# Layer 0's keys, values and context moved into the checks, and layer 2's mixer bias folded into a row

## The chip, the cores and the metric

The kernel runs on one core of one Trainium2 chip. The metric is the device time of one execution in microseconds (us); lower is better. An execution is one launch that computes the whole four-layer network.

## The reference

A graph of 3125 nodes with 256 features each goes through four layers. A layer normalises x, adds a graph attention over some 100,000 edges and a linear "mixer" attention, and then adds a mixture-of-experts block. What matters here is layer 0's mixer and layer 2's sum:

```python
xn = _layernorm(x, axis=-1)
x = x + _L0_gnn_ref(xn, edge_index, ...) + _L0_mix_ref(xn[None], L0_mix_Wqkv, ...)[0]
...
xn = _layernorm(x, axis=-1)
x = x + _L2_gnn_ref(xn, edge_index, ...) + _L2_mix_ref(xn[None], L2_mix_Wq, L2_mix_Wkv, L2_mix_Wproj, L2_mix_bproj)[0]
```

`_L0_mix_ref` takes queries, keys and values from `xn @ Wqkv`, normalises the keys with a softmax over all nodes, forms one context matrix for each head from keys and values, applies it to the queries, multiplies by a gate (a small network on the layer-normalised xn) and projects. The softmax over nodes means that the context needs every node once before any output can be made. `_L2_mix_ref` ends in `einsum(out, Wproj) + bproj`, and `_L2_gnn_ref` ends in a LayerNorm, `... * gamma + beta`. Both are added to the same x.

## The kernel before

The nodes lie in 25 tiles of 125 on the partitions; `GROUPS` joins them to seven groups of four or three tiles. `xn` is the normalised x, `xT` its transpose (features on partitions).

The program has two versions of the network: a fast one (`layers`) and a general one (`general`). Which of the two runs is decided on the chip. `run` loads x, then `begin_layer` normalises all seven groups and transposes them, then `prepare` makes the checks: it counts, for each block of nodes, how many row heads lie before it (five compares over 3224 numbers, L1381), gathers the edge segments with five indirect DMAs on the POOL queue (L1387), builds low digits and keys, writes them to HBM (`seg_d`), tests the sorted edges, the size of the segments, the spread of the attention terms (the `p_e` matmuls over `xT` and the reductions at L1438 and L1439) and the size of Wk. The result is one number, `ok`. It is loaded into registers and a branch follows. What stands before the branch can't be mixed with what stands behind it.

Behind the branch, in `layers`, `counts` builds the matrix of edge counts in 63 steps. In each step DVE makes two one-hot tensors (`oh_lo` L1515, `oh_key` L1518), PE multiplies them (`p_cnt`, L1530, 20 matmuls), and ACT turns the result into bytes (`stage`, L1532), which every fifth step go to HBM (`count_d`, L1536). Beside these steps runs a generator, `mix0_pieces`, with the mixer of layer 0; at each `yield` it hands back. `counts` takes `PIECES0` pieces, spread evenly over the steps, and what is left after the last step follows at once:

```python
while done < (g0 // B + 1) * PIECES0 // steps:
    next(work, None)
    done += 1
```

The pieces before the change are: the weights with the bias add on POOL over the whole x (L1557), then one piece for each tile with its keys and values (`p_a` on PE, Exp and a copy on ACT, a memset of one column on POOL at L1567, and the context matmuls `p_ctx` at L1569), one piece that folds the context into the query weight (`fold`), six for each group (LayerNorm, transpose, gate, fold, projection), and then the node tables of the graph attention (`node_pieces`). That makes 107, which is also `PIECES0`. The dense attention (`dense_pairs`) follows; it reads `count_d` back.

The order on each engine is made by a scheduler at build time from the order in the text (earlier is more urgent) and from what is ready; on the chip each engine and each DMA queue then works in that fixed order. The PE order of the dense attention alone is written out by hand.

In layer 2, `mix2` runs beside the node tables: `keys_values` loops over the 25 tiles (`p_kvt`, `key`, `val`, `p_kv`), and behind it in the text stands the mixer's bias add over the whole x on POOL (L1138). Later `gnn2_out` adds the attention's part to x, with `beta` on POOL (L1120) from a row that `gnn2_weights` loads.

Of the kernel before, what the change touches and what calls it, by code (L numbers as in the profile page):

```python
# [41 lines left out]
KEYS = HI * GN  # L42
PIECES0 = 107
SC = 8
# [12 lines left out]
class Net:  # L57
# [1045 lines left out]
    def gnn2_weights(self, c):  # L1103
        return [self.row(c, "L2_gnn_" + n) for n in ("bias", "gamma", "beta")]

# [18 lines left out]
    def mix2(self, x, xn, xT, work=iter(())):  # L1124
        nc, tc = self.nc, self.tc
        with ExitStack() as s:
            c = s.enter_context(tc.tile_pool(name="m2", bufs=1))
            w = s.enter_context(tc.tile_pool(name="m2w", bufs=2))
            wq, wkv, wproj = (self.weight(c, "L2_mix_" + n) for n in ("Wq", "Wkv", "Wproj"))
            bproj = self.row(c, "L2_mix_bproj")  # L1130

            def finish(out, num, den, z):
                nc.vector.tensor_scalar(z, den, 1e-6, None, op0=OP.max)
                nc.vector.reciprocal(z, z)
                nc.vector.tensor_mul(out, num, z)

            kv, den = self.keys_values(c, w, x, xn, xT, wkv, work)
            nc.gpsimd.tensor_add(x, x, bproj[:, None, :].to_broadcast([TP, NT, C]))  # L1138
# [212 lines left out]
class Dense(Net):  # L1351
# [8 lines left out]
    def prepare(self, pool, xT):  # L1360
# [6 lines left out]
        with ExitStack() as s:  # L1367
# [60 lines left out]
            nc.vector.tensor_reduce(found[:, 1:2], above, AX.X, OP.add)  # L1428
            p_f = ps.tile([1, 2], F32, name="p_f")
            nc.tensor.matmul(p_f, self.ones[:, 0:1], found, start=True, stop=True)  # L1430


            gw = self.gnn_weight(w, ps, "g0", 8)
            ends = w.tile([16, 2, len(GROUPS)], F32, name="ends")
# [30 lines left out]
            nc.vector.tensor_mul(self.ok, ok[:, 0:1], ok[:, 2:3])  # L1465
        return self.ok

# [4 lines left out]
    def counts(self, pieces):  # L1472
# [5 lines left out]
        with ExitStack() as s:  # L1478
# [5 lines left out]
            with tc.tile_pool(name="cnti", bufs=1) as wi, tc.tile_pool(name="cntt", bufs=2, space=PSUM) as ps:  # L1484
                for i, name in enumerate(("lo_t", "key_t")):
# [57 lines left out]
    def mix0_pieces(self, x, xn, xT, nodes, c, w):  # L1543
# [3 lines left out]
        with ExitStack() as s:  # L1547
            ps = s.enter_context(tc.tile_pool(name="m0p", bufs=3, space=PSUM))
            ps1 = s.enter_context(tc.tile_pool(name="m0p1", bufs=1, space=PSUM))
            wqkv = self.weight(c, "L0_mix_Wqkv")  # L1550
            wproj = self.weight(c, "L0_mix_Wproj")
# [3 lines left out]
            bg1, bg2 = self.vec(c, "L0_mix_bg1", rows=64), self.vec(c, "L0_mix_bg2")  # L1555
            bproj = self.row(c, "L0_mix_bproj")
            nc.gpsimd.tensor_add(x, x, bproj[:, None, :].to_broadcast([TP, NT, C]))  # L1557
            p_ctx = [ps1.tile([P, P + 1], F32, name=f"p_ctx{m}") for m in range(KC)]
            yield
            for t in range(NT):  # L1560
                p = ps.tile([TP, 2 * C], F32, name="p_a")
                self.mm(p, [(xT[:, k, t * TP:(t + 1) * TP], wqkv[:, k, C:]) for k in range(KC)])
                ek = w.tile([TP, C], F32, name="ek", bufs=2)
                nc.scalar.activation(ek, p[:, :C], AF.Exp)
                v = w.tile([TP, KC, P + 1], F32, name="v", bufs=2)
                nc.scalar.activation(v[:, :, :P], p[:, C:].rearrange("p (m f) -> p m f", m=KC), AF.Copy)
                nc.gpsimd.memset(v[:, :, P], 1.0)  # L1567
                for m in range(KC):
                    nc.tensor.matmul(p_ctx[m], ek[:, m * P:(m + 1) * P], v[:, m, :], start=(t == 0), stop=(t == NT - 1))  # L1569
                yield  # L1570

            inv = w.tile([P, KC], F32, name="inv")
            ctxt = w.tile([P, KC, P], F32, name="ctxt")
            for m in range(KC):
                nc.vector.reciprocal(inv[:, m:m + 1], p_ctx[m][:, P:])
                nc.vector.scalar_tensor_tensor(ctxt[:, m, :], p_ctx[m][:, :P], inv[:, m:m + 1], self.heads, op0=OP.mult, op1=OP.mult)
            fold = c.tile([P, KC, C], F32, name="fold")
            for k in range(KC):
                p = ps.tile([P, 512], F32, name="p_a")
                for m in range(KC):  # L1580
                    nc.tensor.transpose(p[:, m * P:(m + 1) * P], wqkv[:, k, m * P:(m + 1) * P], self.ident)
                wt = w.tile([P, C], F32, name="wq_t")
                nc.vector.tensor_copy(wt, p[:, :C])
                p = ps.tile([P, 512], F32, name="p_a")
                for m in range(KC):
                    nc.tensor.matmul(p[:, m * P:(m + 1) * P], wt[:, m * P:(m + 1) * P], ctxt[:, m, :], start=True, stop=True)
                nc.vector.tensor_copy(fold[:, k, :], p[:, :C])
            yield
            for t0, nt in GROUPS:
# [876 lines left out]
    def run(self, x_in, out):  # L2466
# [195 lines left out]
```

## Time and profile before

| | us |
|---|---|
| median of 3 runs | 5535.72 (5531.63 to 5546.36) |
| the profiled execution | 5533.53 |
| its span in the trace | 5531.5 |

| stretch of the profiled execution, us | what runs |
|---|---|
| 0 to 32 | x arrives, LayerNorm and transposes |
| 32 to 93 | the checks, up to the branch |
| 93 to 385 | counts with the pieces; first count write issued at 143.4, last at 384.7 |
| 385 to 406 | the last write lands, the node tables are finished, the first loads of the dense attention land |
| 2929 to 3116 | layer 2's mixer beside its node tables |

"Busy" is the time in which an engine worked on an instruction. PE is TensorE, PEld its weight loads, DVE VectorE, ACT ScalarE, POOL GpSimd, SP the queue that issues most DMAs. Lines such as L1530 are lines of the kernel. A name before an arrow is what an instruction writes, the names behind it what it reads. "Granted clock" is the share of its full speed that TensorE was given. Times come from one profiled execution, and a matmul's own duration holds a fixed delay, so dense matmuls are counted by their spacing.

### The profile page before, as it was taken

The page shows a single profiled execution, that of the slowest core. Times are in us where ns is not written, and L with a number is a line of the kernel's source. Part 1 is how long each engine was busy: PE and PEld are TensorE (multiplying, and loading weights), DVE is VectorE, ACT ScalarE, POOL GpSimd, SP SyncE. Part 2 cuts the span into 40 slices and gives each one's busy share as a digit, 9 for nine tenths or more (in the row PEclk, how much of TensorE's full clock was granted, in tenths as well). Part 3 has the DMA queues.
Part 4 walks back from the last instruction along what each step waited for, and adds up shares of the span by engine and source line. Part 5 has one row for each costly group of instructions (what it writes and reads, how often), then busy time and mean ns, then how long its engine had stood idle before and what let it go on. Part 6 is the DMA issues. An engine that isn't in the chain of part 4 may idle for free. (4 is left out here: it accounts for less than half of the span.)

```text
span 5531.5 us, 66568 instructions
## 1 busy us (share of the span) xinstructions
PE 4813.9 (87%) x24758; PEld 2824.0 (51%) x24758; DVE 3733.4 (67%) x5901; ACT 1034.3 (19%) x1984; POOL 1041.6 (19%) x1185
## 2 busy tenths in 40 slices
PE   4978888879788899989889899979998878989878
PEld 2652234448645433368544433345565555655557
DVE  7789999985565699845333899932223888777753
ACT  2540010011142100110123000023333110333221
POOL 1000000004300000000001100000001777777743
PEclk7999999989899999999889999979999888999989
DMA  3462222232300011111000011120002556666645
GB/s 87 36 68 67 77 63 67 67 116 63 99 19 0 27 34 41 32 39 36 24 1 4 28 33 34 26 71 0 0 1 59 161 164 193 183 173 178 175 149 170
DMA packets 294339, 395.81 MB, mean 72 GB/s; under 512 B 124175, under 2 KB 228000, under 8 KB 293435
## 3 DMA queue, kind: packets, MB, share of 16 engines
q1 hardware_dynamic: 203408, 161.12, 12.7%
q0 software_dynamic: 52528, 167.17, 10.7%
q10 hardware_dynamic: 38072, 63.16, 3.6%
q8 instruction: 202, 3.31, 0.3%
q14 instruction: 129, 1.06, 0.1%
HBM read 345.14 MB, written 49.35 MB: 71 GB/s over the span
## 5 line engine op out<-in xcount | busy, mean ns | idle before, releaser
L1699 DVE SCALAR_TENSOR_TENSOR pt<-q_head,bar,a 128x750 f32<-128x750 f32 (+5 forms) x1200 | 1483.3, 1298 | 80.4 <-PE acc L1804 57.3
L1954 POOL DMA_INDIRECT z_edge<-tab,src_i x806 | 778.0, 965 | 266.9 <-issue 206.4
L1748 PE MATMUL acc<-pt,zs 128*64 128x500 f32 (+2 forms) x2800 | 591.1, 548 | 152.0 <-DVE pt L1699 127.2
L1799 PE MATMUL acc<-pt,zs 128*64 128x375 f32 (+2 forms) x3200 | 604.9, 501 | 25.4 <-DVE pt L1699 25.0
L2022 PE MATMUL p_acc<-z_edge,oh 128*125 128x264 f32 x2044 | 539.9, 425 | 91.7 <-DVE z_edge L2013 91.7
L2022 PEld LDWEIGHTS p_acc<-z_edge,oh 128*125 128x125 f32 x2044 | 419.8, 209 | 191.3 <-DVE z_edge L2013 101.2
L1748 PEld LDWEIGHTS acc<-pt,zs 128*64 128x64 f32 (+1 forms) x2800 | 244.4, 136 | 483.3 <-DVE pt L1699 328.7
L1799 PEld LDWEIGHTS acc<-pt,zs 128*64 128x64 f32 (+1 forms) x3200 | 244.9, 136 | 362.0 <-issue 224.7
L1215 DVE SCALAR_TENSOR_TENSOR x<-p_y,sm,x 125x256 f32<-125x256 f32 x200 | 93.9, 484 | 427.0 <-PE p_y L716 427.0
L1804 PE MATMUL acc<-pt,zs 128*32 128x375 f32 (+2 forms) x3200 | 313.4, 497 | 0.0
L1850 PE MATMUL acc<-zs,pt 128*125 128x257 f32 x1250 | 275.7, 383 | 11.8 <-DMA a<-count_d 11.8
L1850 PEld LDWEIGHTS acc<-zs,pt 128*125 128x125 f32 x1250 | 234.8, 189 | 52.7 <-issue 14.6
L2013 DVE TENSOR_TENSOR z_edge<-z_edge,near_e 128x2112 f32<-128x2112 f32 (+1 forms) x101 | 236.5, 2342 | 17.4 <-ACT near_e L2005 17.4
L1210 ACT ACTIVATE h<-p_tr,bn 128x500 f32<-128x500 f32 (+1 forms) x224 | 161.5, 722 | 357.6 <-PE p_tr L716 357.6
L716 PE MATMUL p_y<-w_L_ffn_Wo,h 128*125 128x256 f32 x800 | 203.7, 387 | 0.0
L1699 DVE SCALAR_TENSOR_TENSOR pt<-q_all,bar,a 128x500 f32<-128x500 f32 (+3 forms) x175 | 119.0, 682 | 122.9 <-PE acc L1850 120.4
L716 PE MATMUL p_tr<-h,w_L_ffn_W 128*128 128x500 f32 (+1 forms) x448 | 191.6, 551 | 7.8 <-ACT h L1210 4.7
L2362 POOL CAST one_e<-one 125x96 bf16<-125x96 f32 (+1 forms) x2 | 2.1, 1049 | 1013.5 <-DVE one L653 1013.5
L716 PE MATMUL p_tr<-xT,w_L_ffn_W 128*128 128x500 f32 (+1 forms) x448 | 190.0, 547 | 0.0
L1804 PEld LDWEIGHTS acc<-pt,zs 128*32 128x32 f32 (+1 forms) x3200 | 85.0, 109 | 203.0 <-issue 201.7
L716 PEld LDWEIGHTS p_y<-w_L_ffn_Wo,h 128*125 128x125 f32 x800 | 144.9, 187 | 73.4 <-ACT h L1210 27.1
L1967 DVE TENSOR_TENSOR hot<-row,near 125x1024 f32<-125x1024 int16 (+1 forms) x149 | 157.6, 1083 | 4.5 <-DMA row<-dst_row 2.9
(513 smaller groups left out, 6696.0 us busy)
## 6 DMA issues: line engine op xcount, KB each, us to landing
row<-dst_row SPq DMA_DIRECT2D x101, 224.0 KB
a<-count_d SPq DMA_DIRECT2D x96, 203.1 KB
a<-count_d SPq DMA_DIRECT2D x96, 187.5 KB
a<-count_d SPq DMA_DIRECT2D x144, 93.8 KB
ef<-in_edge_s SPq DMA_DIRECT2D x101, 128.0 KB
z_edge<-tab,src_i POOLq DMA_INDIRECT x806
count_d<-stage SPq DMA_DIRECT2D x12, 781.2 KB
q_head<-q_g ACTq DMA_DIRECT2D x24, 375.0 KB
```

The source lines that it names most:

```text
L716: self.nc.tensor.matmul(p, a, b, start=(i == 0), stop=(i == len(pairs) - 1))
L1210: nc.scalar.activation(o[:, m, :n], p[:, :n], AF.Relu, bias=b[:, e, m:m + 1], scale=g[:, e, m:m + 1])
L1215: nc.vector.scalar_tensor_tensor(x[:, t0 + t, :], q, wf[:, t, e:e + 1], x[:, t0 + t, :], op0=OP.mult, op1=OP.add)
L1699: self.nc.vector.scalar_tensor_tensor(pt[:K, :n], q, bar, a[:K, :n], op0=OP.max, op1=OP.mult)
L1748: nc.tensor.matmul(acc[64 * i:64 * i + 64, :b1 - b0], zs[:K, t, z:z + 64], pts[i][:K, b0:b1], start=(t == 0), stop=(t == NS - 1))
L1799: nc.tensor.matmul(acc[i // 2][64 * (i % 2):64 * (i % 2) + 64, b, :b1 - b0], zs[:K, t, i * W:i * W + 64], pts[i][:K, b0:b1], **st)
L1804: nc.tensor.matmul(acc[2][32 * i:32 * i + 32, b, :b1 - b0], zs[:K, t, z:z + 32], pts[i][:K, b0:b1], **st)
L1850: nc.tensor.matmul(acc[i], pt[:K, i * TP:(i + 1) * TP], zs[:K, t, :C + 1], start=(t == 0), stop=(t == NS - 1))
L1954: nc.gpsimd.indirect_dma_start(out=zs[i][:, j, :], out_offset=None, in_=table, in_offset=bass.IndirectOffsetOnAxis(ap=src[:, c0 + j:c0 + j ...
L1967: nc.vector.tensor_tensor(hots[i, t][:, q0 * 256:q1 * 256], rows[i][:, q0 * 256:q1 * 256], node[:, t:t + 1].to_broadcast([TP, (q1 - q0) * ...
L2013: nc.vector.tensor_mul(zh, zh, weight[:, :, :, None].to_broadcast([P, n, H, D + 1]))
L2022: nc.tensor.matmul(acc[t], ohs[i, t][:, k - a, :], zs[i][:, k - c0, :HW], start=(k == cols[t][0]), stop=(k == cols[t][1] - 1))
```

## The change

Layer 2: the bias of the mixer is added once to the row `beta` (125 partitions x 256) on DVE, and the POOL add over all of x is gone.

Layer 0: a new function `begin` takes the place of `begin_layer` and of the call of `prepare`. `prepare` becomes a generator with three parts, cut behind the gathers and behind the test of the sorted edges. `begin` runs the first part, then goes through the seven groups: transposes of the group, LayerNorm of the next, keys, values and context of its tiles; before the third group's keys it runs the second part of the checks. Then it folds the context, writes the fold to HBM, and runs the rest of the checks. `mix0_pieces` loads the fold from HBM and has 26 pieces fewer (81); `PIECES0` is 69. The scale and shift of `xnnT` go from DVE to ACT. PSUM: `counts` and `mix0_pieces` have four buffers each instead of three (the context had two of its own there before); in the checks `p_f` and `p_gw` share the two buffers of `p_e`.

```diff
-PIECES0 = 107
+PIECES0 = 69
...
     def gnn2_weights(self, c):
-        return [self.row(c, "L2_gnn_" + n) for n in ("bias", "gamma", "beta")]
+        bias, gamma, beta = (self.row(c, "L2_gnn_" + n) for n in ("bias", "gamma", "beta"))
+        self.nc.vector.tensor_add(beta, beta, self.row(c, "L2_mix_bproj"))
+        return bias, gamma, beta
...
-            bproj = self.row(c, "L2_mix_bproj")
...
             kv, den = self.keys_values(c, w, x, xn, xT, wkv, work)
-            nc.gpsimd.tensor_add(x, x, bproj[:, None, :].to_broadcast([TP, NT, C]))
...
                                              in_offset=bass.IndirectOffsetOnAxis(ap=at_i[:, b:b + 1], axis=0))
+            yield
             lo = w.tile([TP, GN, SEG], F32, name="seg_lo")
...
             nc.vector.tensor_reduce(found[:, 1:2], above, AX.X, OP.add)
-            p_f = ps.tile([1, 2], F32, name="p_f")
+            yield
+            p_f = ps.tile([1, 2], F32, name="p_e")
...
-            gw = self.gnn_weight(w, ps, "g0", 8)
+            gw = self.gnn_weight(w, ps, "g0", 8, "p_e")
...
-        return self.ok
+
+    def begin(self, pool, x, xn, xT):
+        nc, tc = self.nc, self.tc
+        self.fold_d = self.dram.tile([P, KC * C], F32, name="fold_d")
+        with ExitStack() as s:
+            c = s.enter_context(tc.tile_pool(name="c0", bufs=1))
+            w = s.enter_context(tc.tile_pool(name="c0w", bufs=2))
+            pst = s.enter_context(tc.tile_pool(name="c0t", bufs=2, space=PSUM))
+            ps = s.enter_context(tc.tile_pool(name="c0p", bufs=2, space=PSUM))
+            ps1 = s.enter_context(tc.tile_pool(name="c0c", bufs=1, space=PSUM))
+            checks = self.prepare(pool, xT)
+            next(checks)
+            wqkv = self.weight(c, "L0_mix_Wqkv")
+            p_ctx = [ps1.tile([P, P + 1], F32, name=f"p_ctx{m}") for m in range(KC)]
+            self.layernorm(xn, x, GROUPS[0])
+            for i, (t0, nt) in enumerate(GROUPS):
+                self.transposed(pst, xT, xn, groups=[GROUPS[i]])
+                if i + 1 < len(GROUPS):
+                    self.layernorm(xn, x, GROUPS[i + 1])
+                if i == 2:
+                    next(checks)
+                for t in range(t0, t0 + nt):
+                    p = ps.tile([TP, 2 * C], F32, name="p_a")
+                    self.mm(p, [(xT[:, k, t * TP:(t + 1) * TP], wqkv[:, k, C:]) for k in range(KC)])
+                    ek = w.tile([TP, C], F32, name="ek")
+                    nc.scalar.activation(ek, p[:, :C], AF.Exp)
+                    v = w.tile([TP, KC, P + 1], F32, name="v")
+                    nc.scalar.activation(v[:, :, :P], p[:, C:].rearrange("p (m f) -> p m f", m=KC), AF.Copy)
+                    nc.gpsimd.memset(v[:, :, P], 1.0)
+                    for m in range(KC):
+                        nc.tensor.matmul(p_ctx[m], ek[:, m * P:(m + 1) * P], v[:, m, :], start=(t == 0), stop=(t == NT - 1))
...
+            nc.sync.dma_start(self.fold_d, fold.rearrange("p k f -> p (k f)"))
+            for _ in checks:
+                pass
...
-            ps = s.enter_context(tc.tile_pool(name="cntp", bufs=3, space=PSUM))
+            ps = s.enter_context(tc.tile_pool(name="cntp", bufs=4, space=PSUM))
...
-            ps = s.enter_context(tc.tile_pool(name="m0p", bufs=3, space=PSUM))
-            ps1 = s.enter_context(tc.tile_pool(name="m0p1", bufs=1, space=PSUM))
-            wqkv = self.weight(c, "L0_mix_Wqkv")
+            ps = s.enter_context(tc.tile_pool(name="m0p", bufs=4, space=PSUM))
...
+            fold = c.tile([P, KC, C], F32, name="fold")
+            nc.sync.dma_start(fold.rearrange("p k f -> p (k f)"), self.fold_d)
             nc.gpsimd.tensor_add(x, x, bproj[:, None, :].to_broadcast([TP, NT, C]))
-            p_ctx = [ps1.tile([P, P + 1], F32, name=f"p_ctx{m}") for m in range(KC)]
-            yield
-            for t in range(NT):
...
-                yield
...
-                    nc.vector.tensor_scalar(xnnT[:, k, :n], p[:, :n], g[:, k:k + 1], b[:, k:k + 1], op0=OP.mult, op1=OP.add)
+                    nc.scalar.activation(xnnT[:, k, :n], p[:, :n], AF.Identity, bias=b[:, k:k + 1], scale=g[:, k:k + 1])
...
-        self.begin_layer(x, xn, xT)
-        ok = nc.values_load(self.prepare(pool, xT)[0:1, 0:1], min_val=0, max_val=1)
+        self.begin(pool, x, xn, xT)
+        ok = nc.values_load(self.ok[0:1, 0:1], min_val=0, max_val=1)
```

The lines left out of `begin` are those of the fold, the same as those removed from `mix0_pieces`.

More of the change, by code (lines that the diff above doesn't have):

```diff
@@ L1465, in prepare @@
             nc.vector.tensor_mul(self.ok, ok[:, 0:1], ok[:, 2:3])
-        return self.ok
+    def begin(self, pool, x, xn, xT):
[28 more added lines that the diff above has]
+                        nc.tensor.matmul(p_ctx[m], ek[:, m * P:(m + 1) * P], v[:, m, :], start=(t == 0), stop=(t == NT - 1))
+            inv = c.tile([P, KC], F32, name="inv")
+            ctxt = c.tile([P, KC, P], F32, name="ctxt")
+            for m in range(KC):
+                nc.vector.reciprocal(inv[:, m:m + 1], p_ctx[m][:, P:])
+                nc.vector.scalar_tensor_tensor(ctxt[:, m, :], p_ctx[m][:, :P], inv[:, m:m + 1], self.heads, op0=OP.mult, op1=OP.mult)
+            fold = c.tile([P, KC, C], F32, name="fold")
+            for k in range(KC):
+                p = ps.tile([P, 512], F32, name="p_a")
+                for m in range(KC):
+                    nc.tensor.transpose(p[:, m * P:(m + 1) * P], wqkv[:, k, m * P:(m + 1) * P], self.ident)
+                wt = w.tile([P, C], F32, name="wq_t")
+                nc.vector.tensor_copy(wt, p[:, :C])
+                p = ps.tile([P, 512], F32, name="p_a")
+                for m in range(KC):
+                    nc.tensor.matmul(p[:, m * P:(m + 1) * P], wt[:, m * P:(m + 1) * P], ctxt[:, m, :], start=True, stop=True)
+                nc.vector.tensor_copy(fold[:, k, :], p[:, :C])
+            nc.sync.dma_start(self.fold_d, fold.rearrange("p k f -> p (k f)"))
+            for _ in checks:
+                pass
@@ L1556, in mix0_pieces @@
             bproj = self.row(c, "L0_mix_bproj")
+            fold = c.tile([P, KC, C], F32, name="fold")
+            nc.sync.dma_start(fold.rearrange("p k f -> p (k f)"), self.fold_d)
             nc.gpsimd.tensor_add(x, x, bproj[:, None, :].to_broadcast([TP, NT, C]))
-            p_ctx = [ps1.tile([P, P + 1], F32, name=f"p_ctx{m}") for m in range(KC)]
-            yield
-            for t in range(NT):
[L1561 to L1569, printed above, removed]
-                yield
[L1572 to L1587, printed above, removed]
             yield
```

## The prediction

> **What bounds the kernel now.** I read the page first. TensorE is the busiest engine over the whole span, but a mean says little here, because the change touches two stretches only: the first 406 us (layer 0 up to the dense attention) and some 200 us of layer 2 near 2930.
>
> ```profile
> PE 4813.9 (87%) x24758; PEld 2824.0 (51%) x24758; DVE 3733.4 (67%) x5901; ACT 1034.3 (19%) x1984; POOL 1041.6 (19%) x1185
> ```
>
> So the second view is the busy time by stretch. The columns are the stretch, its length, busy us of PE, weight loads, DVE, ACT and POOL, the granted TensorE clock, the DMA share and GB/s.
>
> ```profile
> 0.00:13.00 13.00, 0.00 (x0) 0.00 (x0) 6.41 (x38) 2.03 (x4) 3.80 (x58) 1.00 0.90 225
> 13.00:32.00 19.00, 11.22 (x50) 9.00 (x50) 18.67 (x65) 4.91 (x12) 0.00 (x0) 0.82 0.71 164
> 32.00:93.00 61.00, 16.86 (x44) 4.31 (x44) 46.49 (x65) 0.00 (x0) 6.53 (x5) 0.64 0.14 42
> 93.00:132.00 39.00, 22.20 (x84) 12.43 (x85) 28.04 (x65) 14.48 (x35) 16.36 (x10) 0.74 0.33 88
> 132.00:198.00 66.00, 64.26 (x465) 43.04 (x464) 45.58 (x35) 38.67 (x94) 1.92 (x19) 1.00 0.49 37
> 198.00:320.00 122.00, 114.03 (x794) 79.44 (x794) 105.17 (x123) 65.30 (x113) 0.00 (x0) 0.97 0.46 34
> 320.00:385.00 65.00, 62.51 (x542) 46.89 (x541) 58.24 (x70) 41.62 (x98) 0.00 (x0) 1.00 0.65 50
> 385.00:406.00 21.00, 0.00 (x0) 0.00 (x0) 7.28 (x17) 0.00 (x0) 0.00 (x0) 0.58 0.99 86
> ```
>
> From 32 to 93 (the checks) DVE sets the pace and PE is idle for 44 of 61 us; from 132 to 385 (the counts with layer 0's mixer woven in) PE is busy for 240.8 of 253 us and DVE for 209.0. The keys and values sit in the second, the room for them is in the first. The waits of PE from 13 to 93 say the same:
>
> ```profile
> PE p_e L716 <- DVE gw_g L319: 20.6, 1, 20.6
> PE p_f L1430 <- DVE found L1416: 19.7, 1, 19.7
> ```
>
> The groups of the counts stretch (93 to 401) give the prices, as total and mean:
>
> ```profile
> L1518 DVE TENSOR_TENSOR oh_key<-key_t,is_key 128x2520 bf16<-128x2520 bf16 x62 | 99.5, 1607 | 3.5 <-ACT key_t L1497 3.5
> L1515 DVE TENSOR_TENSOR oh_lo<-lo_t,is_lo 128x2560 bf16<-128x2560 bf16 x62 | 92.2, 1489 | 31.2 <-PE p_cnt L1530 29.5 <-ACT lo_t L1497 0.8
> L716 PE MATMUL p_a<-w_L_mix_Wqkv,xT 128*125 128x512 f32 x100 | 50.9, 629 | 0.9 <-DMA v_L_mix_ln_g<-in_L_mix_ln_g 0.9
> L1569 PE MATMUL p_ctx<-v,ek 125*128 125x129 f32 x100 | 17.5, 301 | 9.2 <-POOL v L1567 7.5 <-ACT v L1566 1.0
> ```
>
> DVE's one-hots stood 29.5 us waiting for PE's counting matmuls: PE is the late one there. Last, the order of time in layer 2:
>
> ```profile
> 2929.19 4.56 PE L716 MATMUL p_kvt<-w_L_mix_Wkv,xT 128*125 128x512 f32 x10
> 2931.00 13.66 POOL L1138 TENSOR_TENSOR x<-x,r_L_mix_bproj 125x6400 f32<-125x6400 f32 x1 [2.44 <-DVE xn L619]
> 2931.90 13.38 DVE L726 SCALAR_TENSOR_TENSOR key<-elu_ek,elu_rk 125x256 f32<-125x256 f32 x2 [0.99 <-ACT elu_rk L725]
> 2945.09 1.20 PE L903 MATMUL p_kv<-val,key 125*128 125x129 f32 x4 [11.34 <-DVE key L726]
> ```
>
> Two DVE operations that take 0.42 us each elsewhere end only with POOL's bias add, the memsets of `val` are queued behind that add on POOL, and PE stands still for 11.34 us.
>
> **Layer 2's bias: about -12.5 us.** Removed is one POOL add of 13.66 us. PE's 11.34 us go, and so does the slow start behind them: four p_kv in 1.20 us against 0.67 later, two p_kvt in 1.92 against 1.02, four small ones in 0.81 against 0.51, together 1.7. After it PE is busy for 83.1 of 84 us up to 3029, so the whole 13.0 is on the path, and nothing else is due there: ACT's inputs were ready at 2933.5. Added is one DVE add of two rows 125x256; the nearest row is the 125x256 add into `x`, 0.42 us. It waits for two small row loads that the ACT queue issues near 2928; queued behind it on DVE are the copy of xT and the first `key`. An added operation can't give time back, so it costs between nothing and a 2 us landing; I take 0.5.
>
> **Counts: about -47 us.** Each of 25 tiles takes four p_a matmuls, spaced 0.43 us when dense, and four p_ctx at 0.17: 2.4 us of PE, 60 in all. By 132 some 6.5 tiles were through, so 18.5 tiles (44.4) and the fold (1.5) leave the stretch from 132 to 385; seven of the twelve pieces that now fall behind the loop (69 slots for 81 pieces) take 7 times 0.9 along. PE falls from 240.8 to about 188. DVE loses the scale and shift of xnnT to ACT (14 operations, 9.7 us), the fold's copies (2.6) and 1 us of small copies: 209.0 to 196. DVE is then the bound: a step needs 2.79 us (1.49 and 1.46, slightly overlapped), 63 steps 176. Neither engine ran at 100% beside the other; in 320:385 they stood at 96% and 90%. I take 93% for the busier: 196/0.93 = 211 instead of 253, -42. ACT gains 9 us of xnnT and loses 25 exponentials and copies with four table loads; at under two thirds busy it stays covered. The twelve bursts of count writes each kept the DMA busy for some 10 us every 16 to 29; the step can shrink to 2.8 us (14 a burst) before they bind. In 93:132 PE was blocked by p_ctx for 7.5 us, since the memsets were queued behind layer 0's POOL add (108.88 to 122.56, which stays and still holds one `oh_key` for 10.3 us). Without p_ctx the steady part begins earlier: -5. Bounds: 196 at 100% gives -57 and a start 9 us earlier, -66; at 85% it is 231, -22 and nothing for the start.
>
> **Begin and checks: about +15 us.** The branch on `ok` ends this part at 93 and nothing of the counts passes it. DVE's work hardly changes (2.6 us more); PE's grows by 62. The weight of 768 KB is queued on SP behind x and the row heads; the DMA moved some 280 GB/s from 4 to 20 and was empty from 28, so it costs 2.8 us and the keys start near 27. From there 60 us, 3 for the transposes left, 2 for the cold start and 3 for queues: 95. The queues: POOL's 25 memsets stand among five gathers that wait for `at_i` and take 1.2 to 1.7 us each; ACT's Exp alternates with LayerNorm's Sqrt, 14 table loads of 1.283, 18 us in 68 beside 20 of evictions. Then the last context and fold (2.5) and the seven p_e groups: 16 matmuls at 0.42 and 12 at 0.31, 10.4 us, then reductions and the closing chain (1.2 + 2.7 + 1.1). Wholly behind the keys this is 113; if all but the last group fill gaps earlier, 104. I take 108, so +15. Bounds: +3, if DVE's own chain decides (the row heads at 26, 24 us of cast, compares and what is fitted between them, 12.4 until the gathers land as before, from 53.7 to 66.2, and the 31 us of DVE work behind them: 95 with the copies), to +30, if the compares stand ahead of the LayerNorms and start the keys near 42. The fold's 256 KB go to HBM and back; first use is five pieces into the counts, so it is costed at nothing, and at 3 us if that cover is gone.
>
> **A rule against the move.** Three POOL memsets at 93.7, whose usual time is 0.10, took 1.25 to 1.47 beside a DVE cast of 1.49. The moved memsets stand beside such casts and scalar operations of 0.8 to 1.8 us, so each may wait that long; PE meanwhile has the next tile's p_a (1.72), and I leave the price at zero, 25 x 0.1 at most. The Trainium skill, "SBUF — State Buffer", section "Who interferes with whom", says the port pair that DVE shares with GpSimd is an exclusive lock held for a whole instruction. By that rule alone, 25 waits of up to 1.8 us would be an estimate of 45 us on top.
>
> **Tail: +1 us.** The last count write is issued at 384.7 and the first weighing runs at 406.3. Into these 21.6 us come seven node tiles (some 8) ahead of the 9.4 us of zs products: 17 to 19 in all. At most 4 show.
>
> Sum: -12.5 - 47 + 15 + 1 = -43.5. The profiled execution took 5533.5 (span 5531.5), 2.2 under the median of the runs; against the median 5535.7 this is 5492.
>
> **The rivals.** *The gain is spent before the branch.* If keys, fold and p_e run one after the other and in-order waits on ACT and POOL open holes, the branch comes near 138 (+45): -12.5 - 47 + 45 + 1 = -13.5, or 5522, no measurable change. For it: the closing checks come last in program order. Against: 44 us of idle PE and layer 2's like loop, dense at 2.9 us a tile with more in it. *The keys run at half clock, and it is slower.* In 32:93 the granted clock is 0.64, and at 103 to 106 four p_a took 3.75 us, twice the dense spacing. At that rate 25 tiles cost 120 us, transposes 5, p_e 19 and the close 5: 27 + 149 = 176 for the branch, +83, and the sum is -12.5 - 47 + 83 + 1 = +24.5, or 5560. It decides from a branch at 151 on (+58). For it: that stretch never saw full clock. Against: it had 17 us of work in 61, and the same loop in 2945:3029 was granted 0.98. The Trainium skill, "TensorE: Matmul & The Clock Gate", section "What's actually happening", has the clock halve after an idle window of about 3.4 us and recover after one busy window; by it only the start is slow, an estimated 2 us. *The change does not do what it says*: DVE already is nearly as late as PE in the counts; then only -22 comes there and the sum is -18.5, still inside my range.
>
> **How the numbers follow.** About 0.3% (17 us) is what a measurement tells from no change. Forecast with its sizes, down to -18.5: 0.76. Gain spent: 0.13. Half clock: 0.11. The ends of the forecast are -13 - 66 + 3 = -76 and -11 - 22 + 30 + 4 = +1; that is 5460 to 5537; I keep the low end and cut the high one to 5530, which leaves out the slower rival (0.11), half of the other (0.06) and 0.02 below: 0.19. Faster 0.76, same 0.13, slower 0.11.
>
> **What would show it.** Right: no POOL operation of 13.7 us near 2930 and no gap of PE there; PE busy and a clock near 1.0 from 30 to 95; the branch at 104 to 113; `oh_lo` no longer waiting for p_cnt, DVE above 90% in the counts, the last count write some 240 to 250 us after the branch. Wrong: a branch past 138, or a counts stretch still over 275 us long.

## The result, and the profile after

The changed kernel takes 5508.96 us (median of 6 runs, 5502.20 to 5519.08); the kernel before, in 6 runs beside it, 5533.73. The ratio is 0.9955 with a 95% interval of 0.9945 to 0.9965: 24.8 us faster. The profiled execution took 5502.20 (span 5500.3), 31.3 below the profiled execution of before. The profiled execution of after is the fastest of its six, that of before lies at its median. The forecast was -43.5, so the sign and the range held; the terms behind it fared very differently.

The engines' busy time on the page:

```profile
PE 4824.0 (88%) x24758; PEld 2825.1 (51%) x24758; DVE 3714.3 (68%) x5888; ACT 1047.1 (19%) x2000; POOL 1025.3 (19%) x1184
```

As before the change, the page's means show nothing of it. The stretches do (length, busy us of PE, weight loads, DVE, ACT, POOL, granted clock, DMA share, GB/s):

```profile
0.00:13.00 13.00, 0.00 (x0) 0.00 (x0) 6.95 (x42) 1.96 (x4) 3.87 (x60) 1.00 0.92 238
13.00:32.00 19.00, 12.22 (x41) 7.21 (x42) 18.48 (x40) 4.59 (x8) 0.00 (x0) 0.82 0.78 197
32.00:93.00 61.00, 49.20 (x162) 25.38 (x161) 35.54 (x55) 20.92 (x48) 8.77 (x24) 0.89 0.15 43
93.00:132.00 39.00, 29.41 (x110) 12.28 (x108) 20.27 (x67) 4.47 (x14) 2.84 (x7) 0.92 0.15 33
132.00:198.00 66.00, 44.21 (x320) 30.07 (x321) 59.34 (x75) 35.07 (x71) 13.65 (x1) 0.82 0.34 50
198.00:320.00 122.00, 115.05 (x973) 83.24 (x972) 120.07 (x120) 82.76 (x157) 0.00 (x0) 1.00 0.64 49
320.00:385.00 65.00, 42.03 (x377) 32.31 (x375) 46.82 (x63) 29.71 (x69) 0.00 (x0) 0.87 0.83 86
385.00:406.00 21.00, 15.98 (x62) 5.89 (x62) 20.96 (x16) 0.00 (x0) 0.00 (x0) 0.84 0.29 94
```

From 32 to 93 PE now has 49.2 us of work instead of 16.9, at a granted clock of 0.89 instead of 0.64: the room was used. From 198 to 320 DVE is busy for 120.1 of 122 us (105.2 before), beside 115.1 of PE: the bound has changed hands. From 132 to 198 PE has holes that it did not have before (44.2 us of 66).

The same in marks of the timeline, which every run below shares. "Branch" is the end of the load of `ok`; "first pt" is DVE's first weighing in the dense attention.

| us | before | after | second trace of after |
|---|---|---|---|
| branch | 92.8 | 124.3 | 123.9 |
| first count write | 143.4 | 179.0 | 178.8 |
| last count write | 384.7 | 361.1 | 363.3 |
| first pt | 406.3 | 386.2 | 386.0 |

So layer 0 gives 20.1 us: +31.5 to the branch, +4.1 from there to the first write (50.6, now 54.7), -59.2 from the first to the last write (241.3, now 182.1), +3.5 in the tail (21.6, now 25.1). Layer 2 gives another 11.3 (the same instructions are 20.0 us earlier than before just ahead of it, 31.3 behind it).

What the waits of PE and the groups of the counts look like now; first PE's waits from 13 to 132 (total, times, longest), then two groups from 93 to 401 (total, mean ns of one, idle time before them):

```profile
PE p_ctx L1502 <- POOL v L1500: 5.8, 1, 5.8
PE p_ctx L1502 <- ACT v L1499: 5.5, 1, 5.5
```

```profile
L1571 DVE TENSOR_TENSOR oh_lo<-lo_t,is_lo 128x2560 bf16<-128x2560 bf16 x62 | 91.7, 1481 | 2.2 <-PE p_cnt L1586 2.1
L1574 DVE TENSOR_TENSOR oh_key<-key_t,is_key 128x2520 bf16<-128x2520 bf16 x62 | 90.5, 1461 | 0.0
```

`oh_lo` stood 31.2 us before the change and 2.2 now. The waits for `found` and `gw_g` (20 us each) are gone from the checks, and two new ones of 5.5 and 5.8 have come, both ahead of `p_ctx`. In the timeline of layer 2 the one added operation and the first key products stand where the gap was:

```profile
2915.28 0.42 DVE L1106 TENSOR_TENSOR r_L_gnn_beta<-r_L_gnn_beta,r_L_mix_bproj 125x256 f32<-125x256 f32 x1 [3.38 <-DMA r_L_mix_bproj<-in_L_mix_bproj]
2915.62 0.75 DVE L726 SCALAR_TENSOR_TENSOR key<-elu_ek,elu_rk 125x256 f32<-125x256 f32 x2
2916.19 0.68 PE L903 MATMUL p_kv<-val,key 125*128 125x129 f32 x4 [1.21 <-DVE key L726]
```

The key operations take 0.75 us for two instead of 13.38, and PE waits 1.21 us instead of 11.34. The row add waits for its row's landing. The first `key` is queued behind it on DVE and starts at 2915.6, though the last of its inputs was ready at 2913.1; 1.21 us of that reach PE.

### The profile page after: what moved, and what is told of

Same layout as the page of the kernel before. It is cut to its first block, busy times and chain, and to the rows that moved or that the text cites. A ratio compares the mean times of both kernels' runs of the same rounds, so it can differ in the third digit from the quotient of the medians.

```text
span 5500.3 us, 66547 instructions
## 1 busy us (share of the span) xinstructions
PE 4824.0 (88%) x24758; PEld 2825.1 (51%) x24758; DVE 3714.3 (68%) x5888; ACT 1047.1 (19%) x2000; POOL 1025.3 (19%) x1184
## 5 line engine op out<-in xcount | busy, mean ns | idle before, releaser
L1825 PE MATMUL acc<-pt,zs 128*64 128x375 f32 (+2 forms) x3200 | 605.6, 502 | 25.1 <-issue 14.1
```

Source lines behind the costliest of these rows:

```text
L1825: nc.tensor.matmul(acc[i // 2][64 * (i % 2):64 * (i % 2) + 64, b, :b1 - b0], zs[:K, t, i * W:i * W + 64], pts[i][:K, b0:b1], **st)
```

## The experiments

The experiments ran on four chips. On three of them the last layer, behind 4250 us, takes some 300 us longer in every kernel, the one before included; up to 4200 traces of the same code agree to a few us. So verdicts are read from the marks above, and totals are compared only as ratios to the kernel before on the same chip. An interval behind a ratio is its 95% interval.

**Each part alone.** `e1_row` is the kernel before with the row add of layer 2:

```diff
-        return [self.row(c, "L2_gnn_" + n) for n in ("bias", "gamma", "beta")]
+        bias, gamma, beta = (self.row(c, "L2_gnn_" + n) for n in ("bias", "gamma", "beta"))
+        self.nc.vector.tensor_add(beta, beta, self.row(c, "L2_mix_bproj"))
+        return bias, gamma, beta
...
-            nc.gpsimd.tensor_add(x, x, bproj[:, None, :].to_broadcast([TP, NT, C]))
```

> The kernel before with the change of layer 2 alone. Theory (the POOL add alone made PE's gap of 11.34 us and the slow start behind it, and nothing later absorbs them): the gap near 2930 is gone, the first four p_kv take about 0.68 us instead of 1.20, events behind 2950 are 11 to 12.5 us earlier than before, total -11.5 us (5522 against 5533.7). Rival (a later wait of layer 2, its node tables or its attention's first loads, takes most of it back): events behind 3116 less than 4 us earlier, total within 4 us of before.

Against the trace of before, the instructions ahead of layer 2's mixer are 4.4 us late and those behind it 8.1 us early: -12.5, and it stays (8.1 us early at 3400, 9.0 at 4000). The first key products wait as in the changed kernel:

```profile
2940.39 0.68 PE L903 MATMUL p_kv<-val,key 125*128 125x129 f32 x4 [1.03 <-DVE key L726]
```

The totals alone would not have shown it: ratio 0.9988, interval 0.9973 to 1.0003. The theory holds by the trace, the rival falls.

`e2_layer0` is the changed kernel with that edit taken back, so it holds layer 0's part alone.

> The changed kernel with layer 2's bias add put back on POOL, so layer 0's part alone. Theory (the two parts are independent): branch at 124, dense attention 20 us earlier than before as in the changed kernel's trace, the 11.3 us gap back near 2910, total -18 us with a few us of drift (5512 to 5520 against 5533.7). Rival (layer 0's gain is partly lost later, since the six timed runs of the changed kernel lie 7 us above its profiled one): total -10 or less, with the loss in the stretches behind 400.

Branch 124.0, last write 365.9, first pt 393.0. `e1_row`, on the same chip and with layer 0 as before, has its first pt at 407.9, so layer 0 alone gives 14.9 there, and 0.9977 (0.9964 to 0.9989) in the total. Nothing of it is lost behind 400: the offsets to the trace of before move by about 2 us from 400 to 4000. Against the first trace of the changed kernel it lost 4.8 us between the first and the last write (186.9 instead of 182.1) and 2 in the tail (27.1 instead of 25.1).

`e0_after` is the changed kernel once more.

> The changed kernel itself once more, beside the others. Theory: branch at 124, first count write at 179; the last count write between 361 (its first trace, clock 1.00 throughout the counts) and 366 (the run with layer 0's part alone, clock 0.96 to 0.99 there), so that layer 0's part is worth 15 to 20 us and the sum with layer 2's 11 to 12.5 is -26 to -32 in a trace, -25 in the median. Rival (the 5 us between those two traces come from the order or the code and not from the clock): the last write at 361 again at any clock.

Last write at 363.3, between the two; from the first to the last write it is 184.5. The granted clock from 180 to 300 was 0.97 and 0.99 here, 0.97 and 0.99 in `e2_layer0`, and 1.00 throughout in the first trace of the changed kernel. So a clock below 1.00 goes with a longer stretch, but it does not size it: two traces of equal clock differ by 2.4 us. Total 0.9945 (0.9925 to 0.9965).

**The two holes in the keys.** In the changed kernel's trace, PE between 33 and 61 (start, duration, line, operation, idle time before it):

```profile
33.72 2.74 PE L716 MATMUL p_a<-w_L_mix_Wqkv,xT 128*125 128x512 f32 x6
41.95 1.20 PE L1502 MATMUL p_ctx<-v,ek 125*128 125x129 f32 x4 [5.49 <-ACT v L1499]
42.94 1.92 PE L716 MATMUL p_a<-w_L_mix_Wqkv,xT 128*125 128x512 f32 x2
...
55.46 1.23 PE L1502 MATMUL p_ctx<-v,ek 125*128 125x129 f32 x4 [5.84 <-POOL v L1500]
56.48 1.91 PE L716 MATMUL p_a<-w_L_mix_Wqkv,xT 128*125 128x512 f32 x2
```

The first hole is ACT's queue: a Sqrt for the next group's LayerNorm (`rstd`) stood there ahead of Exp and copy, and waited for DVE, which was in the compares. The second is POOL's queue: two memsets stood behind the five gathers, which began at 47.7, when `at_i` was made, and took until 55.3. The Sqrt, the last gather and the memsets:

```profile
39.54 0.30 ACT L616 ACTIVATE rstd<-mv,eps 125x3 f32<-125x3 f32 x1 [5.41 <-DVE mv L614]
54.08 1.21 POOL L1388 DMA_INDIRECT seg<-in_segments,at_i  x1 [0.30 <-issue]
55.28 0.16 POOL L1500 MEMSET v<- 125x2 f32 x2
```

Behind each hole the rows take nearly twice their dense times (1.20 for 0.68, 1.92 for 1.02); the granted clock is 0.50 to 0.51 from 41.9 to 47 and 0.50 from 55.4 to 59. The second trace has the same two holes with another split, 3.6 and 6.6 us.

`e3_ones` takes POOL out of the loop. The column of ones is set once in two fixed tiles, which the loop uses in turn:

```diff
+            vs = [c.tile([TP, KC, P + 1], F32, name=f"v{i}") for i in range(2)]
+            for v in vs:
+                nc.gpsimd.memset(v[:, :, P], 1.0)
...
-                    v = w.tile([TP, KC, P + 1], F32, name="v")
+                    v = vs[t % 2]
...
-                    nc.gpsimd.memset(v[:, :, P], 1.0)
```

> The changed kernel with two fixed value tiles whose column of ones is set once at the start: no memset on POOL in the key loop. Theory (the memset queued behind the five gathers stopped PE for 5.8 to 6.6 us and the rows behind it ran at half the clock): the hole near 50 to 55 is gone, ACT's hole near 37 to 42 stays, branch at 116 to 118, total 6 to 8 us below the changed kernel. Rival (the next wait in line, the third group's xT behind DVE's casts or ACT's second Sqrt, takes its place): a new hole of 4 us or more before 70 and the branch at 121 or later.

Branch at 117.9 instead of 123.9, first pt at 379.9 instead of 386.0: -6.0, and it stays near that up to 3900 (-5.6 to -7.2). The total is 0.9931 (0.9909 to 0.9954) of the kernel before. The POOL hole is gone; ACT's second Sqrt fills a part of its place:

```profile
42.69 0.71 PE L1504 MATMUL p_ctx<-v,ek 125*128 125x129 f32 x4 [3.76 <-ACT v L1502]
43.23 1.47 PE L716 MATMUL p_a<-w_L_mix_Wqkv,xT 128*125 128x512 f32 x2
...
52.27 0.71 PE L1504 MATMUL p_ctx<-v,ek 125*128 125x129 f32 x4 [2.67 <-ACT v L1502]
52.82 1.02 PE L716 MATMUL p_a<-w_L_mix_Wqkv,xT 128*125 128x512 f32 x2
```

Behind the hole of 2.67 us the matmuls keep their full pace. Behind the one of 3.76 the first four do too (0.71, the granted clock is 1.00 up to 43.2), and then the pace falls: 1.47 instead of 1.02, at a clock of 0.50 from 44.5 to 46.

`e4_ln` keeps the memsets and takes the LayerNorms and transposes out of the loop; the first part of the checks is cut behind its two loads, so that its compares and gathers stand behind them in the text:

```diff
             nc.scalar.dma_start(dst_i, ins["dst_t"])
+            yield
...
-            self.layernorm(xn, x, GROUPS[0])
+            for group in GROUPS:
+                self.layernorm(xn, x, group)
+            self.transposed(pst, xT, xn)
+            next(checks)
             for i, (t0, nt) in enumerate(GROUPS):
-                self.transposed(pst, xT, xn, groups=[GROUPS[i]])
-                if i + 1 < len(GROUPS):
-                    self.layernorm(xn, x, GROUPS[i + 1])
```

> The changed kernel with all LayerNorms and transposes first, as before, then the five compares, then the keys: no group of LayerNorm is left between the compares. Theory (ACT's Sqrt, in order ahead of Exp and copy, stood behind DVE's compares and stopped PE for 5.5 us, and the cold rows behind it cost 2 more): no Sqrt on ACT between the Exps, no hole of PE near 36 to 42, ACT's table loads in the stretch down from 8 to about 2; the gathers are issued some 5 us later (53 instead of 47.7), the POOL hole of 5.8 us stays behind them; branch at 117 instead of 124.3, total 6 to 7 us below the changed kernel (-31 against before). Rival (the wait is only moved: the later gathers hold POOL's memsets, and so PE, longer): the POOL hole grows to 10 us or more and the branch stays within 2 us of 124.3.

The rival's mechanism holds, at the edge of its marks: the branch is 2.0 us below 124.3, and the POOL hole grew to 8.7 us, not to 10. No Sqrt is left between the Exps and no hole over 0.6 us before 50, but the gathers move from 48.0 to 51.4 and the memsets behind them hold PE for longer:

```profile
59.13 1.23 PE L1503 MATMUL p_ctx<-v,ek 125*128 125x129 f32 x4 [8.67 <-POOL v L1501]
```

Branch at 122.3, 1.7 us before that of `e2_layer0` on the same chip; first pt at 391.6, 1.4 sooner; total 0.9956 (0.9941 to 0.9971). With the ACT hole closed the work ran into the POOL hole sooner; both had to go.

**Who bounds the counts.** `e6_dve` puts the scale and shift of `xnnT` back on DVE:

```diff
-                    nc.scalar.activation(xnnT[:, k, :n], p[:, :n], AF.Identity, bias=b[:, k:k + 1], scale=g[:, k:k + 1])
+                    nc.vector.tensor_scalar(xnnT[:, k, :n], p[:, :n], g[:, k:k + 1], b[:, k:k + 1], op0=OP.mult, op1=OP.add)
```

> The changed kernel with the scale and shift of xnnT back on DVE (14 operations of about 0.69 us, 9.7 us). Theory (DVE is the bound of the counts now, at 98 of 100): the last count write 7 to 10 us later than in the changed kernel, total +7 to +10 against it. Rival (PE with its 92 to 95 of 100 and the waits between the two set the pace, DVE's share only looks full): last write within 3 us, total within 3 us.

9.7 us of work moved to DVE made the last write 9.3 us later than in `e0_after` (372.6 for 363.3) and the first pt 9.6 (395.6 for 386.0); 0.9 of it is a later branch, so 8.4 behind the branch. The total is 0.9964 (0.9946 to 0.9981), 8.4 us above the changed kernel on that chip. The window from 198 to 320:

```profile
198.00:320.00 122.00, 111.75 (x916) 81.56 (x915) 119.10 (x124) 70.92 (x135) 0.00 (x0) 0.99 0.53 47
```

PE has less to do in it than in any trace of the changed kernel (111.8 us for 115), DVE is as full as there, and the stretch is longer: DVE is the bound. Three traces of layer 0 unchanged differ by up to 4.8 us in this stretch, so that most of the 9.7 us came through is shown, the exact share is not.

**Layer 0's bias add.** It stays on POOL at the start of the counts. In the trace after, POOL's line and DVE's beside it:

```profile
136.94 13.65 POOL L1613 TENSOR_TENSOR x<-x,r_L_mix_bproj 125x6400 f32<-125x6400 f32 x1 [9.39 <-DMA r_L_mix_bproj<-in_L_mix_bproj]
```

```profile
137.66 14.05 DVE L619 TENSOR_SCALAR xnn<-xn,mv,rstd 125x256 f32<-125x256 f32 x4
```

Four scalings that take 1.38 us in the next group take 14.05, and the first one alone 13.08. `e5_bias0` gives the bias to PE (the row is then loaded to one partition):

```diff
-            nc.gpsimd.tensor_add(x, x, bproj[:, None, :].to_broadcast([TP, NT, C]))
...
+                        self.mm(p[:, i, :], [(gate[:, m, (t + i) * TP:(t + i + 1) * TP], wproj[:, m, :]) for m in range(KC)]
+                                + [(self.ones[:1, :TP], bproj)])
```

> The changed kernel with layer 0's bias taken into the projection as a third matmul (a row of ones by the bias row) in place of the POOL add over x. Theory (DVE's four scalings xnn took 14.05 us instead of 1.4 because they stood still beside POOL's add of 13.65, and all of the counts' start is behind them): the four take 1.4 to 1.6 us, the first count write comes 43 us after the branch instead of 54.7, the 25 extra matmuls (6 us of PE at about 0.25) are hidden since DVE is the bound of the counts; total 8 to 13 us below the changed kernel (about -36 against before). Rival (the first steps wait for the segment loads and their transposes, which end at 157 anyway): the first count write stays 52 us or more behind the branch, total within 3 us of the changed kernel.

The four scalings take 1.35 us, and the first write comes 42.5 us behind the branch, as expected, 12.5 sooner than in `e2_layer0` on the same chip. But the last write is only 5.7 sooner (360.2) and the first pt 6.2 (386.8): the stretch between the writes grew from 186.9 to 193.6. Against the two traces of the changed kernel itself, on other chips, the first pt is no sooner at all (386.2 and 386.0), and the total, 0.9969 (0.9955 to 0.9984), is what the two parts give together on this chip (0.9988 and 0.9977). So the 8 to 13 us that were expected did not come. The window from 198 to 320 and the group of the new matmuls (from 180 to 360) say why:

```profile
198.00:320.00 122.00, 119.67 (x948) 82.27 (x947) 113.36 (x112) 73.07 (x143) 0.00 (x0) 1.00 0.64 47
```

```profile
L716 PE MATMUL p_a<-r_L_mix_bproj,ones 1*125 1x256 f32 x42 | 14.5, 425 | 0.0
```

Two rows that follow each other give the price of one product by the spacing:

```profile
230.92 0.69 PE L716 MATMUL p_a<-r_L_mix_bproj,ones 1*125 1x256 f32 x2
231.54 1.13 PE L716 MATMUL p_a<-w_L_mix_Wproj,gate 128*125 128x256 f32 x4
```

PE is at 98% and DVE back at 93%. The 25 products are 50 instructions (42 of them between 180 and 360), and one product takes 0.62 us of PE, so 25 take some 15.5, where the expectation had 6; PE had only 6 us in a hundred to spare.

**A better version.** `e8_best` joins the edits of `e3_ones` and `e4_ln` and moves the POOL add into DVE's idle time in the checks. There `next(checks)` hands back one column of `rel`, which the casts write, so that the row `late` can't be made before them:

```diff
+                    zero = c.tile([TP, 1], F32, name="zero")
+                    nc.vector.tensor_scalar(zero, next(checks), 0.0, None, op0=OP.mult)
+                    late = c.tile([TP, C], F32, name="late")
+                    nc.vector.tensor_scalar(late, bproj, zero[:, 0:1], None, op0=OP.add)
+                    nc.gpsimd.tensor_add(x, x, late[:, None, :].to_broadcast([TP, NT, C]))
...
-            nc.gpsimd.tensor_add(x, x, bproj[:, None, :].to_broadcast([TP, NT, C]))
```

> The changed kernel with three things at once: fixed value tiles (no POOL memset in the key loop), all LayerNorms and transposes ahead of the compares (no Sqrt between the Exps), and layer 0's bias add on POOL moved from the start of the counts into the idle DVE time of the checks, behind the casts (two small DVE operations make its row wait for them). Theory: keys without a hole from 29 to 94, then fold, p_e and the close, 17 us: branch at 110 to 112; POOL's add from 76 to 90 beside an idle DVE; first count write 43 us after the branch, steady part 182 to 187 as before; last write at 335 to 342, total 22 to 27 us below the changed kernel, about -50 against the kernel before. Rival (PE is behind DVE by little only, as when 25 extra matmuls took half of a 12 us gain back): the steady part grows by what the start loses, total 10 to 15 us below the changed kernel.

Its window over the key loop, and POOL's add in its new place:

```profile
30.00:93.00 63.00, 61.77 (x213) 29.45 (x212) 39.28 (x40) 19.12 (x53) 20.41 (x6) 1.00 0.14 42
```

```profile
78.14 13.73 POOL L1501 TENSOR_TENSOR x<-x,late 125x6400 f32<-125x6400 f32 x1 [18.18 <-DVE late L1500]
```

PE is busy for 61.8 of 63 us at a clock of 1.00. Against `e0_after`: branch 113.1 (10.8 sooner, 1.1 past the mark of 112), first write 41.9 behind it, last write 336.9 after 181.9 us more, first pt 360.1 (25.9 sooner; 23.2 are left near 4200). The other marks are met. Ratio 0.9913 (0.9886 to 0.9940): 5763.58 against 5788.58 for the changed kernel on that chip, 25.0 below it. By the totals alone the two intervals overlap; the marks decide.

**The tail.** At the end of the counts ACT takes exponentials of `es`, and DVE multiplies the node tables `zs` by them (the zs products, 8.0 us). In the trace after, ACT's exponential stands for 11.5 us, and the products begin only behind it:

```profile
376.94 0.37 ACT L1694 ACTIVATE bar<-es 128x200 f32<-128x200 f32 x1 [11.47 <-DMA count_d<-stage]
```

It is queued on ACT behind the first issue of the `q_head` load, at 376.53, and that one waits for transfers to land; the `es` that the exponential reads was whole at 365.7. `e7_pieces` sets `PIECES0 = 81`.

> The changed kernel with PIECES0 = 81, so that no piece is left for behind the loop. Theory (the tail grew because the two exponentials of es stand on ACT behind the q_head loads, which wait for the last write of q_g: the zs products begin at 378 instead of 363, and the first pt is DVE's at 386 instead of 382): the exponentials run before the last count write, the first pt comes 21 to 22 us after that write as in the kernel before (25 in the changed kernel's first trace, 22.7 in its second); the seven node tiles cost the loop 0 to 4 us of PE, which is at 92 to 95 of 100; total between -4 and +1 against the changed kernel. Rival (PE then binds the counts as with the 25 extra matmuls): last write 5 us or more later, total +2 or more.

Neither side is right as written: the last write meets the rival's mark, the first pt does not. The products now stand between the one-hots, and the last write is 5.5 us later than in `e0_after` (368.8); the first pt then comes 15.3 us behind it, at 384.1, 1.9 sooner:

```profile
361.98 1.45 DVE L1574 TENSOR_TENSOR oh_key<-key_t,is_key 128x2520 bf16<-128x2520 bf16 x1
363.36 0.97 DVE L1700 TENSOR_TENSOR zs<-zs,es 128x800 f32<-128x800 f32 x1
363.49 2.32 PE L1586 MATMUL p_cnt<-oh_key,oh_lo 128*128 128x125 bf16 x20 [2.44 <-DVE oh_key L1574]
```

The ratio is 0.9921 (0.9907 to 0.9934). The changed kernel itself has no run on that chip, and the marks give 1.9 us, so how much of this ratio is due to the 81 is not shown. `e9_best81` is `e8_best` with 81:

> The version with three edits (fixed value tiles, LayerNorms and transposes first, layer 0's bias add in the checks) and PIECES0 = 81. Theory: as for the changed kernel: first pt 21 to 22 us after the last write instead of 23.2, last write 0 to 4 us later than 336.9; total within 4 us of the version with 69, on either side. Rival (PE binds, 95 of 100 before the node tiles are added): last write at 342 or later, total +3 or more against the version with 69.

Last write 343.7, first pt 359.2 for 360.1; within the 4 us that were expected, though the rival's mark for the last write was met. It has the lowest ratio of all, 0.9896 (0.9881 to 0.9911; 5478.23 against 5540.77), but its interval overlaps that of `e8_best`. `e11_pieces77` and `e10_best77` set 77 in the changed kernel and in the better version, so that the products stay behind the last one-hots:

> The changed kernel with PIECES0 = 77 and nothing else. Theory: last write at 361 to 365 as with 69, first pt at 378 to 382 instead of 386, total 4 to 8 us below the changed kernel (some 30 us below the kernel before). Rival (the node tiles alone make PE late): last write at 367 or later, first pt at 384 or later as with 81.

> The version with three edits and PIECES0 = 77: node tiles and the two exponentials inside the loop, the zs products (four pieces) behind the last one-hots. Theory (with 81 the products stood ahead of the last one-hots on DVE and moved the last write by 5 to 7 us; with 69 the exponentials stood behind the q_head loads): last write at 337 to 340, products while it lands, first pt 15 to 21 us behind it at 353 to 358, total 2 to 6 us below the version with 81. Rival (the node tiles alone make PE late): last write at 342 or later, first pt at 359 or later, no gain against 81.

The theory fails in both. The rival holds in the better version and is missed by a hair in the changed kernel (366.6 for 367): last write 366.6 and 343.7, first pt 384.0 and 362.3, ratios 0.9939 (0.9916 to 0.9962) and 0.9914 (0.9886 to 0.9941). The products do stand behind the one-hots, and still the last write is only 2.2 us sooner than with 81 in the changed kernel and no sooner in the better version, and the first pt is no sooner in either. Between 240 and 300, with 77 in the changed kernel and in the better version:

```profile
240.00:300.00 60.00, 58.41 (x497) 43.45 (x496) 59.60 (x61) 42.72 (x82) 0.00 (x0) 1.00 0.48 45
240.00:300.00 60.00, 59.38 (x510) 45.19 (x509) 58.80 (x63) 39.09 (x85) 0.00 (x0) 1.00 0.64 56
```

With 69 PE had 55.7 and 57.6 us there. With the node tiles inside, both engines are full, so what leaves the tail comes back in the loop.

## Why the prediction was right, and where it was not

**Layer 2, -12.5.** Right, by its mechanism too: -11.3 in the trace after, -12.5 alone. The 0.5 us set for the row's landing measured 1.2 as a wait of PE.

**Begin and checks, +15.** Wrong, and past its bound of +30: +31.5 (31.1 in the second trace). The keys started at 27.0 as worked out and ran at 2.45 us a tile, but the last context came near 107.5 instead of 95. The step that failed is "3 for queues". Both queues had been named (memsets among the gathers, Exp alternating with Sqrt) and set at 3 us together; they measured 5.5 and 5.8, plus the slow rows behind each. On ACT it is not the length of what is issued (a Sqrt of 0.30 us) but the 5.4 us that the Sqrt ahead waited for DVE. On POOL it is the five gathers in a row, 7.6 us, which could begin only when `at_i` was there, in the midst of the key loop; the two memsets behind them take 0.16. (The 14 table loads counted there were 7.) The bounds named the compares only as a delay of the start, not in the midst of the loop. The second failed choice was 108 between 104 and 113: fold, p_e and close all ran behind the last context, 16.7 us, where the text had 2.5 + 10.4 + 5. The version without either hole reached its branch at 113.1, the prediction's own figure for p_e wholly behind the keys. The rival "gain spent before the branch" had this mechanism; at 124 the branch had come about half of the way from the 108 of the forecast to its 138. The half clock of the other rival appeared only for some microseconds behind each hole (0.50 up to 47 and up to 59).

**Counts, -47.** The sum was near (-55.1; -52.5 and -50.0 in the two other traces), the parts were not. From the first write to the last it was -59.2: DVE became the bound, as forecast, and `e6_dve` shows it, but at 98% and not at 93%; 196/0.98 is 200 us and -53 instead of 211 and -42. (The text cut the counts at 132 and not at the first write, at 143.4, so its two parts compare only roughly with these.) Which share the fourth PSUM buffer has in it, no run isolates. The start was +4.1 instead of -5. The text had let POOL's add hold one `oh_key` for 10.3 us as before; it now met the scalings that PE's queue waited for, and the memsets' 7.5 us that left were not what came last there. `e5_bias0` puts that hold at 12.5 us.

**Tail, +1.** +3.5 in this trace, +1.1 in the second, both inside the "at most 4"; in `e2_layer0` +5.5, or +4.1 against `e1_row` on its chip. It was not by the length of the work that the text added up (the products take 8.0 us and not 9.4, since they overlap a little): an exponential of 0.37 us was queued on ACT behind a load that waits for a landing.

**The marks.** Seen: no POOL operation and no gap near 2930, `oh_lo` without its wait, DVE over 90%. Missed: clock near 1.0 and PE busy from 30 to 95 (0.89, with two holes), branch at 104 to 113. The last write came 236.8 us behind the branch, 239.4 in the second trace and 241.9 in `e2_layer0`, for 240 to 250.

**The sum.** 31.5 - 55.1 + 3.5 - 11.3 = -31.4, which is the profiled executions' difference, against -43.5. The 12 us between are the begin's excess of 16.5, less the counts' 8, plus tail and layer 2 (4). That the total stayed inside the range is in part luck: a term past its own bound was made up for by one that came out 8 us better, for a reason (98%) that the text had only as a bound. That the median moved by 24.8 and not by 31.3 stays open: the two profiled executions were still 27.9 us apart near 4200, layer 0's part was 15 to 20 us in three traces, and runs of one kernel differ by 17 us.

**The rule weighed.** The 25 memsets took 3.15 us in all, 0.10 each but for one of 0.67; the price of zero was right for them, and the 45 us did not come. (Of the three memsets at 93.7 that the text gives as usually 0.10, the widest takes 0.34 elsewhere.) The Trainium skill, "SBUF — State Buffer", section "Who interferes with whom", has the lock held for a whole instruction; the scaling of 13.08 us beside one POOL add of 13.65 agrees with it. Without that add, in `e5_bias0`, the same four scalings took 1.35. So in these rows the length of the one instruction that holds the lock decides, and a rule that seemed to speak against the memsets spoke against the add that the change left where it was.

## What to carry to other kernels

When work is moved beside other work, do not price an in-order queue by the length of the instruction that is added to it: for each engine, ask what stands ahead of it, when that can begin, and how long the whole row of it takes. Two holes with different causes hide each other: closing the POOL one alone brought the branch 6.0 us forward, the ACT one alone 1.7, both 10.8. When the bound passes to a second engine and the first is only a few per cent behind it, look at what an edit adds to the first: 25 small products on PE took back at least half of 12.5 us, and pieces moved from the tail into the loop cost there most of what the tail saved, in one case more.

## What the runs showed of the hardware that was not expected

- One POOL add over 125x6400 floats (13.65 us) held a DVE scaling of 0.4 us for 13.08 us. In the kernel before, BATCH_NORM_STATS2 took its usual 0.40 us beside the same add, so not every DVE operation is held.
- PE's pace after a hole: unchanged after 2.67 us, up to twice as slow for some microseconds after 3.76, 5.49, 5.84 and 8.67; after 3.76 it began only half a microsecond into the work. The Trainium skill, "TensorE: Matmul & The Clock Gate", section "What's actually happening", puts the idle window at about 3.4 us; the runs lie on both sides of it and agree, with a single hole on the lower side.
- DVE ran at 98% over 120 us beside a PE at 94%; 93% was thought to be the most.
